# Projections of an attention kernel as four column-group products each, and the first key block's product in two halves

## The chip, the cores and the metric

The kernel runs on one core of a Trainium2 chip. The metric is the device time of one execution in microseconds; the median of three executions of the kernel before is 1588.9 us. Every profile and every time in this document is of that one core.

## What is computed

The reference is one "macaron" layer on an input of 8 sequences of 1024 tokens and 256 features, in float32: half a feed-forward block with experts, causal attention with 16 heads of 16 features, and another half feed-forward block, each behind a layer norm.

```python
x = L0_attn_x                                   # (8, 1024, 256)
x = x + 0.5 * _L0_ffn_ref(_layernorm(x, axis=-1), gate_w, w1, b1, w2, b2)
x = x + _L0_attn_ref(_layernorm(x, axis=-1), Wq, bq, Wkv, bkv, Wo, bo)
x = x + 0.5 * _L0_ffn_ref(_layernorm(x, axis=-1), gate_w, w1, b1, w2, b2)

def _L0_attn_ref(x, Wq, bq, Wkv, bkv, Wo, bo):
    q = x @ Wq.T + bq
    k, v = jnp.split(x @ Wkv.T + bkv, 2, axis=-1)
    q, k, v = (to_heads(q), to_heads(k), to_heads(v))
    dots = jnp.einsum('bhid,bhjd->bhij', q * scale, k)
    dots = jnp.where(causal, MASK_VAL, dots)
    attn = jax.nn.softmax(dots, axis=-1)
    out = jnp.einsum('bhij,bhjd->bhid', attn, v)
    return out.transpose(0, 2, 1, 3).reshape(b, n, d) @ Wo.T + bo

def _L0_ffn_ref(tokens, gate_w, w1, b1, w2, b2):
    cap = int(1.25 * N / E)
    probs = softmax(x @ gate_w.T); top2_w, top2_idx = top_k(probs, 2)
    counts = jnp.bincount(top2_idx.reshape(-1), length=E)
    keep = counts <= cap
    ...
```

An expert that is chosen more often than its capacity allows is dropped as a whole. The kernel counts the choices of both feed-forward blocks while it computes the attention, and works out a feed-forward block only in a branch that is taken where some expert is kept.

## The kernel before

In this profile the whole span is one call of `attention` (line 602). Its work is cut into 32 units: a unit `u` is one sequence `b` and one group `g` of four heads (`u = 4 b + g`). The loop at line 966 takes 24 steps for each unit. In every step TensorE gets, in this order:

- a score block (lines 991 to 996): two products `sc` of the unit `u` (keys against queries, for the exponential) interleaved with two products `sm` of the next unit (queries against keys, for the row maximum). All four contract 16 features in one of four row groups of 32 partitions, so that they run in the array at the same time; the profile writes this as 32*128. They are 512, 384, 256 or 128 columns wide. There are six PSUM banks for them (`score`, line 616), used in turn: a step's third product needs the bank that the first `sc` of the step before had, and its fourth the bank of the first `sm` of the step before. ScalarE (ACT) releases the first by its `Exp` into `pT`, VectorE (DVE) the second by its maximum.
- what is due of the products with v (lines 998 to 1003): `values(hf, jb, pTs, part)` (line 816). A product `pav` multiplies the exponentials of key block `jb` with v, four heads at once, each in one of four column groups of 32 output rows (128*32 in the profile). It is due two steps after its scores (`part` 0) and three steps after (`part` 1). Blocks of over 256 columns are divided in two parts, except for the first key block, whose 512 columns are all done in part 0; blocks of up to 256 columns are done in part 0 too. In the numbering of steps from 0 to 23, the first key block of the unit's first half of queries comes at step 3, that of the second half at step 11.
- one piece of other work (lines 1015 to 1022): at steps 2 and 12 `settle`, with four transposes `pm`; else the next piece of a queue, `even` at even steps and `odd` at odd ones.

The pieces of the two queues are made by generators. `enter` makes transposes `pta` of the normed input, `values_of` (line 678) one product `pv` a piece for v and the gate (264 columns, contracted over 256 features in two halves `c`), `project` (line 718) one product `pq` a piece for the keys or the queries of eight heads (512 columns, again two halves), and `leave` (line 860) one product `px` a piece for the output projection and the second gate (264 columns, two halves). These three kinds of projection use the full array of 128 by 128; so do the transposes. All of `pav`, `pv`, `pq`, `px`, `pm` and `pta` share the two PSUM banks of `bank` (line 620), one of which `pav` holds for about half a unit. A float32 product of TensorE shows as two weight loads and two matmuls in the trace.

The order of each engine's instructions is kept as written by `InOrder` (line 27), whose call at line 37 is why nearly all rows of the profile name line 37.

Of the kernel before, what the change touches and what calls it, by code (L numbers as in the profile page):

```python
# [18 lines left out]
P = 128  # L19
# [31 lines left out]
def macaron_kernel(  # L51
# [550 lines left out]
    def attention(run_no, src, dst, gate0, logits, tally):  # L602
# [3 lines left out]
        with stack:  # L606
# [20 lines left out]
            def matmul(out, lhsT, rhs, start=True, stop=True):  # L627
                pe.matmul(out, lhsT=lhsT, rhs=rhs, start=start, stop=stop)

            def transpose(out, in_, n=P):  # L630
                pe.transpose(out, in_, ident[:n, :n])

            xbs, xnTs, lns, stds, att_ds, qEs, gate_lns = {}, {}, {}, {}, {}, {}, {}


# [42 lines left out]
            def values_of(b):  # L678
                xb, xnT = xbs[b], xnTs[b]
                if gate0 is None:  # L680
                    lg = norm.tile([P, TB, E], F32, tag="lg", name=f"lg{b}")
                else:
                    lg = gate0[0][:, b * TB : (b + 1) * TB, :]
                for j in range(TB):
                    pv = bank(f"pv{b}_{j}")
                    for c in range(DC):
                        matmul(
                            pv[:, : D + E],
                            xnT[:, c, j * P : (j + 1) * P],
                            wvT[:, c, :],  # L690
                            start=(c == 0),
                            stop=(c == DC - 1),
                        )
                    vector.tensor_tensor(
                        vaugs[b % 2][:, j, : NH * VW].rearrange("p (h r) -> p h r", r=VW)[:, :, :HD],
                        pv[:, :D].rearrange("p (h r) -> p h r", r=HD),
                        bv_all.rearrange("p (h r) -> p h r", r=HD),
                        ALU.add,
                    )
                    vector.tensor_copy(lg[:, j, :], pv[:, D : D + E])  # L700
                    yield
                gpsimd.tensor_tensor(
                    xb[:, :, D:], lg, stds.pop(b).unsqueeze(2).to_broadcast([P, TB, E]), ALU.mult
                )
                for j in range(0, TB, 2):
                    part = xb[:, j : j + 2, :]
                    gpsimd.tensor_tensor(part, part, bo_all.unsqueeze(1).to_broadcast([P, 2, D + E]), ALU.add)
                    yield
# [9 lines left out]
            def project(u):  # L718
                b, g = divmod(u, NG)
                xnT = xnTs[b]  # L720
                gp = g // 2
                for s0 in range(0, S, 512):
                    for wT, bT, dsts, scale in ((wkT, bkT, kTs, 1.0), (wqT, bqT, qTs, QSCALE)):
                        pq = bank(f"pq{u}_{s0}")
                        for c in range(DC):
                            matmul(
                                pq,
                                wT[:, c, gp * P : (gp + 1) * P],
                                xnT[:, c, s0 : s0 + 512],
                                start=(c == 0),  # L730
                                stop=(c == DC - 1),
                            )
                        packed = ap.tile([P, 512], F32, tag="packed", name=f"packed{u}_{s0}", bufs=4)
                        scalar.activation(packed, pq, AF.Identity, bias=bT[:, gp : gp + 1], scale=scale)
                        for k in range(8):
                            r = 32 * (k % 4)
                            nc.sync.dma_start(  # L737
                                out=dsts[(u + k // 4) % 4][r : r + HD, s0 : s0 + 512],
                                in_=packed[HD * k : HD * (k + 1), :],
                            )  # L740
                        yield
# [44 lines left out]
            def e_steps(u):  # L786
                b, g = divmod(u, NG)
                kT = kTs[u % 4]
                pav = {}

                def scores(hf, jb, pr, out, h):
                    off = max(0, jb - 4 * hf) * P
                    w = 512 - off
                    r = 64 * pr + 32 * h
                    sc = score(f"sc{u}_{hf}_{jb}_{pr}_{h}")
                    matmul(sc[:, :w], kT[r : r + 32, jb * P : (jb + 1) * P], qEs[u, hf][r : r + 32, off:])
                    if h == 0:
                        out[pr] = ap.tile([P, 2, 512], F32, tag="pT", name=f"pT{u}_{hf}_{jb}_{pr}", bufs=8)
                    pT = out[pr]
                    scalar.activation(pT[:, h, :w], sc[:, :w], AF.Exp)  # L800
                    if h == 0:
                        return
                    if jb >= 4 * hf:
                        gpsimd.affine_select(
                            out=pT[:, :, :P],
                            in_=pT[:, :, :P],
                            pattern=[[0, 2], [1, P]],
                            compare_op=ALU.is_ge,
                            fill=0.0,
                            base=0,  # L810
                            channel_multiplier=-1,
                        )

                def values(hf, jb, pTs, part):
                    if jb == 0 and part == 0:
                        pav[hf] = bank(f"pav{u}_{hf}")
                    off = max(0, jb - 4 * hf) * P
                    w = 512 - off  # L820
                    if jb == 0 or w <= 256:
                        cols = slice(0, w)
                        if part == 1:
                            return
                    else:
                        cols = slice(part * w // 2, (part + 1) * w // 2)
                    for pr in (1, 0):
                        for h in range(2):
                            r = 64 * pr + 32 * h
                            v0 = (4 * g + 2 * pr + h) * VW  # L830
                            matmul(
                                pav[hf][r : r + 32, off + cols.start : off + cols.stop],
                                vaugs[b % 2][:, jb, v0 : v0 + 32],
                                pTs[pr][:, h, cols],
                                start=(jb == 0),
                                stop=(jb == 4 * hf + 3),
                            )
                    if jb == 4 * hf + 3 and part == 0:
                        att = ap.tile([P, 512], F32, tag="att", name=f"att{u}_{hf}", bufs=4)
                        scalar.copy(att, pav.pop(hf))  # L840
                        if g == 0:
                            att_ds[b, hf] = spill.tile(
                                [NH, 32, 512], F32, tag="att_d", name=f"att_d{run_no}_{b}_{hf}", bufs=3
                            )
                        nc.sync.dma_start(
                            out=att_ds[b, hf][4 * g : 4 * g + 4].rearrange("h r c -> (h r) c"), in_=att
                        )

                for hf in range(2):
                    for jb in range(4 * hf + 4):  # L850
                        pTs = {}
                        yield (lambda h, hf=hf, jb=jb, pTs=pTs: scores(hf, jb, 1, pTs, h)), None
                        yield (
                            (lambda h, hf=hf, jb=jb, pTs=pTs: scores(hf, jb, 0, pTs, h)),
                            (lambda part, hf=hf, jb=jb, pTs=pTs: values(hf, jb, pTs, part)),
                        )
# [3 lines left out]
            def leave(b, hf):  # L860
# [29 lines left out]
                for i in range(TB // 2):  # L890
                    j = hf * (TB // 2) + i
                    px = bank(f"px{b}_{j}")
                    for c in range(DC):
                        matmul(
                            px[:, : D + E],
                            on[:, c, i * P : (i + 1) * P],
                            woT[:, c, :],
                            start=(c == 0),
                            stop=(c == DC - 1),
                        )  # L900
                    vector.tensor_tensor(xb[:, j, :], px[:, : D + E], xb[:, j, :], ALU.add)
                    ln_stats(xb, j, *gate_lns[b])
                    yield
# [192 lines left out]
```

## Time and profile before

| | |
|---|---|
| median of three runs (lowest, highest) | 1588.9 us (1586.56, 1589.5) |
| the profiled execution's own time | 1588.83 us |
| its span, from the first to the last instruction | 1587.1 us |
| mean granted TensorE clock | 0.966 |
| matmuls of TensorE, and their weight loads | 11940 each |

The groups with the largest busy time of TensorE's projections and products with v, kept apart by shape (columns: line, engine, operation, output <- inputs, array tile, shape, count | busy us, mean ns of one | idle time before):

```profile
L37 PE MATMUL pav<-pT,vaug 128*32 128x256 f32 x2560 | 204.7, 391 | 0.0
L37 PE MATMUL pav<-pT,vaug 128*32 128x512 f32 x512 | 71.6, 632 | 0.1
L37 PE MATMUL pq<-xnT,wkT 128*128 128x512 f32 x128 | 63.5, 619 | 0.0
L37 PE MATMUL pq<-xnT,wqT 128*128 128x512 f32 x128 | 63.3, 617 | 0.0
L37 PE MATMUL pv<-wvT,xnT 128*128 128x264 f32 x256 | 76.3, 422 | 7.2 <-DVE logits L37 4.1 <-DVE xa L37 3.2
L37 PE MATMUL px<-woT,on 128*128 128x264 f32 x256 | 75.4, 419 | 16.3 <-POOL on L37 16.3
```

How to read it: matmuls run at the same time in different tiles and overlap in the pipeline, so a group's busy time is the time in which at least one of its matmuls is in the array[...]. Neither is the time that a block of matmuls costs. For that, the timeline is needed: the distance from the start of a block's first matmul to the start of the next block's first.

### The profile page before, as it was taken

What the parts mean: (1) busy time and instruction counts of PE and PEld (TensorE: products, weight loads), DVE (VectorE), ACT (ScalarE), POOL (GpSimd) and SP (SyncE); (2) the same over time, 40 slices, a digit from 0 to 9 for tenths busy, and PEclk for the clock granted to TensorE, in tenths of its full rate; (3) what the DMA queues carried; (4) which work ended last, traced back from release to release, by engine and by line L of the source; (5) the groups of instructions that cost most, each with busy time, mean ns of one, the idle gap of its engine ahead of it and who ended that gap; (6) DMA issues with size and microseconds to landing.
All of it is one profiled execution on the core that took longest, in us unless ns stands there. A gap on an engine that the chain in (4) does not pass through costs nothing.

```text
span 1587.1 us, 32518 instructions
## 1 busy us (share of the span) xinstructions
PE 1496.4 (94%) x11940; PEld 630.2 (40%) x11940; DVE 1120.9 (71%) x3519; ACT 764.3 (48%) x1722; POOL 332.6 (21%) x650
## 2 busy tenths in 40 slices
PE   4999999999999999999999999999999999999992
PEld 2444444344344434444344443334334443344431
DVE  4576777676867678676876768677686767767823
ACT  1045555454554455553554545554455535555560
POOL 3111212112121121223121131211212221112121
PEclk9779999999999999999999999999999999999996
DMA  4001111111111020211212111110302101121111
GB/s 126 13 14 28 37 32 45 46 36 54 55 50 49 27 74 23 61 49 32 64 34 56 36 49 52 50 49 21 87 22 62 42 23 46 36 62 36 34 36 57
DMA packets 58056, 71.69 MB, mean 45 GB/s; under 512 B 15640, under 2 KB 33312, under 8 KB 57888
## 3 DMA queue, kind: packets, MB, share of 16 engines
q1 hardware_dynamic: 55680, 68.20, 14.4%
q8 instruction: 96, 1.57, 0.4%
q10 hardware_dynamic: 2208, 1.32, 0.3%
q14 instruction: 72, 0.59, 0.1%
HBM read 27.01 MB, written 25.69 MB: 33 GB/s over the span
## 4 chain that ended last, share of the span: by engine, by line
PE 90%; DVE 6%; issue 1%; DMA 1%; SPq 1%; POOL 1%; ACT 0%; ACTq 0%; POOLq 0%
PE sc L37 39%; PE pav L37 20%; PE sm L37 10%; PE pq L37 7%; PE pv L37 5%; PE px L37 4%; PE pm L37 2%; DVE sm L37 2%; PE pta L37 1%; DVE first L37 1%; DVE xn_a L37 1%; SPq L737 1%; DMA xa<-in_L_attn_x_dram 0%; ACT pT L37 0%; DMA inv<-inv_d 0%
## 5 line engine op out<-in xcount | busy, mean ns | idle before, releaser
L37 ACT ACTIVATE pT<-sc 128x512 f32<-128x512 f32 (+3 forms) x1536 | 670.1, 490 | 637.1 <-PE sm L37 484.4
L37 PE MATMUL sm<-kT,qT 32*128 32x512 f32 (+3 forms) x3072 | 847.6, 545 | 13.7 <-DVE top L37 7.2
L37 PE MATMUL sc<-qE,kT 32*128 32x512 f32 (+3 forms) x3072 | 784.0, 541 | 1.0
L37 POOL TENSOR_SCALAR_AFFINE_SELECT pT<-pT 128x256 f32<-128x256 f32 x512 | 208.2, 408 | 1110.5 <-ACT pT L37 1106.6
L37 PEld LDWEIGHTS sc<-qE,kT 32*128 32x128 f32 x3072 | 285.7, 185 | 331.0 <-ACT pT L37 201.8
L37 DVE TENSOR_REDUCE first<-sm 128x1 f32<-128x512 f32 x512 | 329.1, 685 | 111.9 <-PE sm L37 99.5
L37 PE MATMUL pav<-pT,vaug 128*32 128x256 f32 (+3 forms) x4608 | 373.4, 396 | 0.1
L37 DVE CUSTOM_DVE_ANT_0 sm<-sm,causal 128x256 f32<-128x256 f32 (+3 forms) x512 | 241.5, 515 | 165.7 <-PE sm L37 164.9
L37 PEld LDWEIGHTS sm<-kT,qT 32*128 32x128 f32 x3072 | 329.3, 187 | 52.8 <-issue 18.5
L37 DVE CUSTOM_DVE_ANT_0 sm<-sm,causal,first 128x256 f32<-128x256 f32 (+3 forms) x512 | 261.7, 553 | 46.7 <-PE sm L37 31.0
L37 PEld LDWEIGHTS pav<-pT,vaug 128*32 128x32 f32 x4608 | 91.4, 108 | 298.9 <-issue 227.6
L37 DVE DVE_READ_ACCUMULATOR2_ANT top<- 128x1 f32 x1024 | 145.2, 142 | 0.0
L37 PE MATMUL px<-woT,on 128*128 128x264 f32 x256 | 75.4, 419 | 16.3 <-POOL on L37 16.3
L37 PE MATMUL pv<-wvT,xnT 128*128 128x264 f32 x256 | 76.3, 422 | 7.2 <-DVE logits L37 4.1
L37 DVE TENSOR_TENSOR xa<-px,xa 128x264 f32<-128x264 f32 x64 | 27.6, 432 | 58.3 <-PE px L37 56.5
L37 PE MATMUL pq<-xnT,wkT 128*128 128x512 f32 x128 | 63.5, 619 | 0.0
L37 PE MATMUL pq<-xnT,wqT 128*128 128x512 f32 x128 | 63.3, 617 | 0.0
L37 PEld LDWEIGHTS px<-woT,on 128*128 128x128 f32 x256 | 44.4, 193 | 47.3 <-POOL on L37 18.2
L37 PEld LDWEIGHTS pv<-wvT,xnT 128*128 128x128 f32 x256 | 44.7, 194 | 41.7 <-issue 10.9
L37 DVE TENSOR_TENSOR vaug<-pv,bv_all 128x256 f32<-128x256 f32 x64 | 27.1, 424 | 30.2 <-PE pv L37 28.8
L37 PE MATMUL pta<-ident,xn_a 128*128 128x128 f32 x128 | 23.2, 310 | 25.4 <-DVE xn_a L37 25.4
L37 DVE TENSOR_TENSOR qE<-qT,pm 128x512 f32<-128x512 f32 x64 | 43.6, 682 | 3.6 <-PE pm L37 3.6
(108 smaller groups left out, 595.3 us busy)
## 6 DMA issues: line engine op xcount, KB each, us to landing
att_d<-att SPq DMA_DIRECT2D x64, 256.0 KB
xa<-in_L_attn_x_dram SPq DMA_DIRECT2D x8, 1024.0 KB
kT<-packed SPq DMA_DIRECT2D x256, 32.0 KB
qT<-packed SPq DMA_DIRECT2D x256, 32.0 KB
on<-att_d SPq DMA_DIRECT2D x32, 256.0 KB
inv<-inv_d SPq DMA_DIRECT2D x32, 256.0 KB
out_dram<-xa SPq DMA_DIRECT2D x16, 512.0 KB
wsb<-in_L_attn_Wkv_dram ACTq DMA_DIRECT2D x2, 256.0 KB
```

Source lines behind the costliest of these rows:

```text
L37: i = call(*args, **kwargs)
L737: nc.sync.dma_start(out=dsts[(u + k // 4) % 4][r : r + HD, s0 : s0 + 512], in_=packed[HD * k : HD * (k + 1), :],)
```

## The change

A helper `matmul_cols` is added that issues a product as four, each for 32 of the 128 output rows; the four write the same PSUM bank at partitions 0, 32, 64 and 96. The three kinds of projection call it in place of `matmul`. In `values`, the first key block of 512 columns is no longer taken whole in part 0: columns 0 to 255 are done in part 0 and columns 256 to 511 in part 1, one step later; only part 0 carries the start flag.

```diff
+            def matmul_cols(out, lhsT, rhs, start=True, stop=True):
+                for r in range(0, P, 32):
+                    matmul(out[r : r + 32], lhsT[:, r : r + 32], rhs, start, stop)
...
                     for c in range(DC):
-                        matmul(
+                        matmul_cols(
                             pv[:, : D + E],
                             xnT[:, c, j * P : (j + 1) * P],
                             wvT[:, c, :],
...
                         for c in range(DC):
-                            matmul(
+                            matmul_cols(
                                 pq,
                                 wT[:, c, gp * P : (gp + 1) * P],
                                 xnT[:, c, s0 : s0 + 512],
...
                 def values(hf, jb, pTs, part):
...
-                    if jb == 0 or w <= 256:
+                    if w <= 256:
                         cols = slice(0, w)
                         if part == 1:
                             return
...
-                                start=(jb == 0),
+                                start=(jb == 0 and part == 0),
                                 stop=(jb == 4 * hf + 3),
...
                     for c in range(DC):
-                        matmul(
+                        matmul_cols(
                             px[:, : D + E],
                             on[:, c, i * P : (i + 1) * P],
                             woT[:, c, :],
```

TensorE's program grows by 1152 float32 products for the projections (192 projections of two halves, three more products for each half) and by 256 for the divided key block (two halves of queries in 32 units, four heads each). The instructions of the other engines and their order stay as they are.

## The prediction

> **What bounds the kernel now.** I read the page first, part 1 for the busy shares and part 4 for the chain, then the groups kept apart by shape, then TensorE's timeline.
>
> ```profile
> PE 1496.4 (94%) x11940; PEld 630.2 (40%) x11940; DVE 1120.9 (71%) x3519; ACT 764.3 (48%) x1722; POOL 332.6 (21%) x650
> PE 90%; DVE 6%; issue 1%; DMA 1%; SPq 1%; POOL 1%; ACT 0%; ACTq 0%; POOLq 0%
> PE sc L37 39%; PE pav L37 20%; PE sm L37 10%; PE pq L37 7%; PE pv L37 5%; PE px L37 4%; PE pm L37 2%; DVE sm L37 2%; PE pta L37 1%; DVE first L37 1%; DVE xn_a L37 1%; SPq L737 1%; DMA xa<-in_L_attn_x_dram 0%; ACT pT L37 0%; DMA inv<-inv_d 0%
> ```
>
> TensorE is the bound, and all three projections lie on the chain nearly whole: 7 + 5 + 4% of 1587 us is 254 us. [...] I need the distance from the first matmul of a block to the first of the next. The timeline gives it:
>
> ```profile
> 720.92 0.64 PE L37 MATMUL pav<-pT,vaug 128*32 128x256 f32 x8
> 721.49 1.16 PE L37 MATMUL px<-woT,on 128*128 128x264 f32 x4
> 722.58 0.58 PE L37 MATMUL sc<-qE,kT 32*128 32x384 f32 x1
> ...
> 646.47 1.06 PE L37 MATMUL pav<-pT,vaug 128*32 128x512 f32 x8
> 647.47 0.48 PE L37 MATMUL sc<-qE,kT 32*128 32x256 f32 x1
> ...
> 648.11 1.98 PE L37 MATMUL pq<-xnT,wqT 128*128 128x512 f32 x4
> 650.03 0.48 PE L37 MATMUL sc<-qE,kT 32*128 32x256 f32 x1
> ```
>
> A full-array px takes 1.09 us (721.49 to 722.58), a pq 1.92, four column-group products of 256 columns 0.57, of 512 columns 1.00. I took these distances over the whole trace, sorted by what stands before and after; they repeat to 1 or 2 ns: pav 356, 462, 569 and 996 ns for 128, 192, 256 and 512 columns; pv and px 1087; pq 1914.
>
> Every float32 product is two passes. The pav row is 139 ns + two passes of 1.67 ns a column (2 x 429 at 512, 2 x 215 at 256). For pq, 1914 = 198 + 4 x 429, with 429 the distance between its second, third and fourth matmul; for px, 1087 = 199 + 4 x 222. So four column groups stream at the full array's rate, all four at once, and the block's fixed part is 139 ns against 199.
>
> [...] a score block (32x128 tiles) between others costs 1070 ns, while one followed directly by another score block costs 962[...]. [...] In the trace the second pass starts 533 ns after the first in a 512-column score block (107 over the 427 of streaming), 453 in pav (26 over). [...]
>
> **The change part by part.**
>
> 1. Projection directly behind a pav in the same step. [...] Afterwards both have one mode and the projection should cost only its streaming, 4 x 222 = 888 or 4 x 429 = 1716: a gain of 199 each. Nearest row for such a chain: two score blocks with no other block between, where a tile's next product starts 429 ns after its last pass, nothing exposed. Counted in the program's order: 59 px, 36 pv, 17 pq = 112. 112 x 0.199 = 22.3 us.
>
> 2. Projection behind a score block: 199 becomes 139, 60 ns each. pq: 43 today, of which 14 get a pav ahead by part 4, so 29 x 0.06 = 1.7 us. pv: 8 x 0.06 = 0.5.
>
> 3. The six places at a unit's end where two pv follow px and wait for a bank (VectorE releases it): each starts its streaming 80 ns sooner, 12 x 0.08 = 1.0 us. The first four pq, the eight pv ahead of the first scores and the last four px stand beside VectorE and DMA waits; I take 0, at most 1 us.
>
> Does the gain survive? A score block's third matmul waits for ACT's exp of the score block before, its fourth for VectorE's reduction: the stall is set by the filler between two score blocks. In the trace, no filler gives a stall of about 860 to 970 ns at 512 columns, 586 ns of filler 270, 996 ns none. All fillers with a projection are at least 1.02 us afterwards, and today every score block after one has a stall of 0 to 2 ns. So the gain stays on the path. VectorE could come in where both takes of a step pair hold projections: in the unit at 719.85 to 734.10 it is busy 10.81 of 14.25 us, against six gains of 0.2.
>
> 4. The first key block's pav, 996 ns at steps 3 and 11 of a unit, becomes 569 there and 569 at steps 4 and 12, so TensorE pays 142 more; stalls move too. Cases over 31 units, sums of the two fillers and the stalls behind them (ns):
> - step 4 with nothing (10 units): before 996 - 108[...] + 764 = 1652; after 569 + 200 + 569 + 75 = 1413. Gain 0.24 each, 2.4 us. The 200 is ACT's and VectorE's 384-column work not yet done after 569 (the row with 586 before such a block has 204 to 207).
> - step 4 with pq (14): before 996 + 1914 = 2910; after 569 + 200 + 569 + 1716 = 3054. Loss 0.144, 2.0 us.
> - step 4 with pta (7): before 996 + 586 + 70 = 1652; after 569 + 200 + 569 + 585 = 1923. Loss 0.27, 1.9 us.
> - step 11 without px (23): before 996 + 586 (pm) + 270 = 1852; after 569 + 270 + 569 + 585 = 1993. Loss 0.14, 3.2 us. The transposes of pm come 142 ns later; the qE that VectorE makes of them is not read for ten steps.
> - step 11 with px (7), its 199 counted in 1: the pm stall of 270 goes, 142 is added. Gain 0.13, 0.9 us.
> Sum: a loss of 3.8 us.
>
> VectorE's, ACT's, POOL's and SP's instructions and their order are the same; pT of key block 0 is held one step longer, with eight buffers and one used a step, which costs nothing.
>
> Bounds for what the trace does not show. The chain pav to projection: full gain 22.3[...]. Sixteen column products reading one moving operand in four streams: pav's four streams are different data, so equality is not shown; I take equality. The split: at best the stall after step 3 is 0 (6 us better), at worst VectorE lags and it is 427 (7 us worse). I take the middle.
>
> Net: -22.3 - 1.7 - 0.5 - 1.0 + 3.8 = -21.7 us. The span 1587.1 becomes 1565.4, and the profiled execution's own time 1588.83 becomes 1567.1; the median of the runs, 1588.9, is the same to 0.1.
>
> **Rivals.**
>
> A, the gain is halved. For: with VectorE 71% busy and no idle time in some steps (2, 3 and 13 of many units), a step shortened by 0.2 hands part of it to the next stall; and matmuls come denser. [...] afterwards steps with 128-column scores, pav and pv hold 32 matmuls in about 1.78 us, 56 ns each. Against: pav of 128 columns already has eight in 356 ns, 45 each, and 512-column steps are at 79. Price: some 10 us, 1577.
>
> B, slower. Each burst of four column products pays the block's fixed part for itself, because the second half of the sum (c = 1) writes the bank's same rows as the first. Then a pv or px is 2 x (139 + 444) = 1166 instead of 1087, a pq 2 x (139 + 858) = 1994 instead of 1914: +0.08 on some 190 projections, 15 us, and the split loses its shared mode with 14 pq (+2.8 over 3.8): 1588.8 + 15 + 6.6 = 1610. It decides against the change from an extra 0.12 us per projection on (21.7 / 188). For it: no column chain over eight products is in the trace. Against: the score chain of eight products, and the second pass in each pav, which adds to the same rows 429 ns after the first.
>
> C, the change doesn't do what it says: four products with the same moving operand run one after the other. Then pv and px grow by 3 x 888 and pq by 3 x 1716 ns: 128 x 2.66 + 64 x 5.15 = 670 us, about 2260. Against: the four tiles of pav start 7 ns apart.
>
> **How the numbers follow.** Forecast 0.66 (own range 1559 to 1575), A 0.16, B 0.13, C 0.01, and 0.04 that gains and losses cancel. A measurement of this kernel tells about 0.2% (3 us) from no change. Faster: forecast and A, 0.82; same 0.04; slower 0.14. Range 1559 to 1582 takes in A and the unknown ends.
>
> **What would show it.** Distance from px to the next score block behind a pav near 890 ns, pq near 1716; pq behind scores near 1855. Steps 4 and 12 with a pav of 569; stall at step 12 near 270 and at 13 near 0. A first matmul of c = 1 more than 240 ns after the second pass of c = 0 in the same group shows B. Stalls over 50 ns behind projections show A. If the px blocks come out at 890 and the time has not fallen by 15 us, my reading of the stalls is wrong.

## The result, and the profile after

The changed kernel takes 1573.6 us (median of ten, 1564.49 to 1578.89) against 1588.5 for the kernel before; the ratio is 0.9889, with a 95% interval from 0.9852 to 0.9926. The profiled execution took 1565.43 us, its span is 1563.7 us at a mean granted clock of 0.968. The ten executions fall into two groups, five from 1564.5 to 1569.3 us at a clock of 0.965 to 0.968 and five from 1577.9 to 1578.9 at 0.958 or 0.959, so the profile stands for the faster group and the median lies between the two (experiment 4 asks what separates them).

Page of the kernel after, part 1 and both lines of part 4:

```profile
PE 1473.4 (94%) x14756; PEld 601.3 (38%) x14756; DVE 1124.1 (72%) x3519; ACT 764.4 (49%) x1722; POOL 333.3 (21%) x650
PE 89%; DVE 7%; issue 1%; DMA 1%; SPq 1%; POOL 1%; ACT 0%; ACTq 0%; POOLq 0%
PE sc L37 40%; PE pav L37 21%; PE sm L37 10%; PE pq L37 7%; PE pv L37 4%; PE px L37 4%; PE pm L37 2%; DVE sm L37 2%; PE pta L37 1%; DVE first L37 1%; DVE xn_a L37 1%; SPq L743 1%; DMA xa<-in_L_attn_x_dram 0%; DVE key_g L37 0%; DVE cand_g L37 0%
```

2816 more matmuls, and TensorE is busy for 23 us less. The shares of the chain are nearly those of before: the bound did not move, it became cheaper. Where, the timeline of TensorE in the kernel after shows (start us, length us, engine, line, operation, count):

```profile
711.23 0.64 PE L37 MATMUL pav<-pT,vaug 128*32 128x256 f32 x8
711.69 1.07 PE L37 MATMUL px<-woT,on 128*32 128x264 f32 x16
712.69 0.58 PE L37 MATMUL sc<-qE,kT 32*128 32x384 f32 x1
...
638.04 0.64 PE L37 MATMUL pav<-pT,vaug 128*32 128x256 f32 x8
638.49 1.90 PE L37 MATMUL pq<-xnT,wqT 128*32 128x512 f32 x16
640.33 0.48 PE L37 MATMUL sc<-qE,kT 32*128 32x256 f32 x1
```

From pav to the next score block it is now 1.46 us with a px between (1.66 before), and 2.29 with a pq. The px starts only 0.46 us after pav where it was 0.57. Score blocks of 512 columns show nearly the same step in the trace of before: 962 ns where another score block follows directly, 1070 where a block of another mode does. A mode here is the array tile that the profile prints, such as 128*32.

Executions also differ in how long TensorE ran at half clock; a stretch in which the trace shows a granted clock of 0.5 is called a dip below. To compare kernels without the dips I use a second number, the undisturbed time of units 2 to 30. It is the sum, over these units, of the distance from the unit's first score matmul to that of the next unit. A unit that a dip touches counts with the median of the untouched units of the same `g` in sequences 1 to 6 (of 0 to 7); these agree within 0.02 us, though in some traces only one of a `g` is untouched. The undisturbed time is 1318.6 us before and 1297.8 after, 20.8 less. Units 0 and 1 hold dips of nearly the same length in both traces and add 1.9, so the gain in units 0 to 30 is 22.7 us. To take off half of every dip instead would mislead: in units 5, 9 and 25 of the kernel before, 6.8 us at half clock cost 2.57 us and not 3.4, since TensorE waits in part of them anyhow.

### The profile page after: what moved, and what is told of

It is laid out like the page before. It is cut to its first block, busy times and chain, and to the rows that moved or that the text cites. A ratio compares the mean times of both kernels' runs of the same rounds, so it can differ in the third digit from the quotient of the medians.

```text
span 1563.7 us, 38156 instructions
## 1 busy us (share of the span) xinstructions
PE 1473.4 (94%) x14756; PEld 601.3 (38%) x14756; DVE 1124.1 (72%) x3519; ACT 764.4 (49%) x1722; POOL 333.3 (21%) x650
## 4 chain that ended last, share of the span: by engine, by line
PE 89%; DVE 7%; issue 1%; DMA 1%; SPq 1%; POOL 1%; ACT 0%; ACTq 0%; POOLq 0%
PE sc L37 40%; PE pav L37 21%; PE sm L37 10%; PE pq L37 7%; PE pv L37 4%; PE px L37 4%; PE pm L37 2%; DVE sm L37 2%; PE pta L37 1%; DVE first L37 1%; DVE xn_a L37 1%; SPq L743 1%; DMA xa<-in_L_attn_x_dram 0%; DVE key_g L37 0%; DVE cand_g L37 0%
## 5 line engine op out<-in xcount | busy, mean ns | idle before, releaser
L37 PE MATMUL pav<-pT,vaug 128*32 128x256 f32 (+2 forms) x5120 | 385.7, 373 | 0.1
L37 PEld LDWEIGHTS pav<-pT,vaug 128*32 128x32 f32 x5120 | 101.3, 108 | 334.4 <-issue 259.1
L37 PE MATMUL px<-woT,on 128*32 128x264 f32 x1024 | 70.8, 396 | 16.2 <-POOL on L37 16.2
L37 PE MATMUL pv<-wvT,xnT 128*32 128x264 f32 x1024 | 71.6, 398 | 7.7 <-DVE logits L37 4.3
L37 PE MATMUL pq<-xnT,wkT 128*32 128x512 f32 x512 | 61.8, 601 | 0.0
L37 PE MATMUL pq<-xnT,wqT 128*32 128x512 f32 x512 | 61.1, 595 | 0.0
L37 PEld LDWEIGHTS px<-woT,on 128*32 128x32 f32 x1024 | 33.1, 112 | 39.7 <-POOL on L37 18.3
L37 PEld LDWEIGHTS pv<-wvT,xnT 128*32 128x32 f32 x1024 | 31.3, 111 | 42.0 <-issue 7.1
L37 ACT ACTIVATE packed<-pq,bqT 128x512 f32<-128x512 f32 x32 | 22.0, 687 | 47.5 <-PE pq L37 38.5
```

The lines of the kernel that those rows point to most:

```text
L37: i = call(*args, **kwargs)
```

## The experiments

**1. The two parts of the change, each alone.** The first kernel keeps the column groups and leaves the first key block's product whole:

```diff
-                    if w <= 256:
+                    if jb == 0 or w <= 256:
...
-                                start=(jb == 0 and part == 0),
+                                start=(jb == 0),
```

> Projections in column groups, first key block's product left whole. Theory (the gain is the shared tiling mode[...]): 112 projections behind a pav save 0.199 us, 51 behind scores 0.060, the pairs at a unit's end 1.0 in all: a span 26.4 us under that of before, 1560.7. A px behind a pav adds 890 ns to it, a pq behind scores takes 1855. Rival (the divided key block brings a good part of the gain, by filling steps that had no filler): a span over 1570.

The second is the kernel before with those two lines the other way, and its projections in the full array.

> First key block's product divided, projections left in the full array. Theory: 62 times 142 ns more of TensorE time, stalls that move rather than go, and no shared mode with the pq of step 4: 3 to 7 us slower than before, a span of 1590 to 1594. Rival (dividing evens out the steps): faster than before by 3 us or more.

Column groups alone: 1571.2 us, ratio 0.991 (0.9878 to 0.9941), profiled span 1569.5 at a clock of 0.961. In the trace every block is as expected: px adds 890 ns to a pav (456 + 1003, against 569), a pq behind scores takes 1854. But the span is 9 us over the forecast and, read alone, within 0.5 us of what the rival said. Most of that is the clock: there are ten dips between 150 and 1520 us, where before has seven. Set against untouched units, the dips of units 2 to 30 cost 15.3 us here and 13.0 before, and unit 0, which holds dips in both, lasts 2.7 us longer. The undisturbed time is 1296.6, 22.0 under before, with units 0 and 1 some 24 (an estimate, as the dips in unit 0 differ); 26.4 were expected for the whole span. The divided block alone: 1593.3 us, ratio 1.0024 (1.0002 to 1.0046), a profiled span of 1594.5, just over the range given, and an undisturbed time of 1321.8, 3.2 over before. So the column groups bring the whole gain and the divided block costs. Alone it costs 3.8 us by its own timed runs (0.24% of 1589) and 3.2 undisturbed. Beside the column groups it costs 1.2 (1297.8 - 1296.6), because the 14 pq at step 4 then stand behind a pav and save 198 ns instead of 60. The timed runs of the first kernel and of the change itself overlap and do not rank these two.

**2. Shared mode or short weight loads.** Two products of 64 rows in place of four of 32:

```diff
-                for r in range(0, P, 32):
-                    matmul(out[r : r + 32], lhsT[:, r : r + 32], rhs, start, stop)
+                for r in range(0, P, 64):
+                    matmul(out[r : r + 64], lhsT[:, r : r + 64], rhs, start, stop)
```

> As the change, but each projection as two products of 64 output rows, which is another tiling mode than that of pav (four groups of 32). Theory (most of the gain is the mode shared with pav): [...] fixed part near 150 ns in place of 199, so about 8 us gained on the projections and 6 lost on the divided block: a span of 1583 to 1588. Rival (the gain is the shorter weight load and the overlap of groups, in any column mode): a span under 1575.

In the traces a weight load of px lasts 190 ns before and 110 after (medians). Measured: 1572.2 us, ratio 0.9922 (0.9892 to 0.9951), a profiled span of 1569.9. By the time alone, both theories miss and the rival's is the nearer. TensorE's timeline of this kernel says otherwise:

```profile
713.37 0.64 PE L37 MATMUL pav<-pT,vaug 128*32 128x256 f32 x8
713.93 1.11 PE L37 MATMUL px<-woT,on 128*64 128x264 f32 x8
714.98 0.58 PE L37 MATMUL sc<-qE,kT 32*128 32x384 f32 x1
```

The pav ahead of px is back at 0.56 (0.57 before, 0.46 in the change) and px costs 1041 ns, 153 + 888, where the forecast, an estimate of mine, was "near 150". Counted by kind of block outside the dips (the median distance of each kind, times how often it stands there), the projections gain 46 or 47 ns each, 7.8 us in units 0 to 30, where four groups gain 26.6. The undisturbed time is 1314.8, 3.8 under before, so the divided block takes back about half of the 7.8. The rest of the time came from elsewhere: this execution has a single dip of the clock between 110 and 1500 us, before has eight, and those of units 2 to 30 cost it 13.0 us. So a column mode other than pav's is worth 7.8 us here; the mode shared with pav carries most of the other 18.8, since a projection behind a pav keeps a fixed part of 153 ns with 64 rows and, with 32, costs its streaming alone (890 ns for a px that streams 888). That its clock is better is not explained by the edit; 11 of its 17 executions are at 0.975 or above, those of before and after at 0.955 to 0.971.

**3. The order of the small products.** The loop over row groups outside, the two halves of the sum inside:

```diff
-                for r in range(0, P, 32):
-                    matmul(out[r : r + 32], lhsT[:, r : r + 32], rhs, start, stop)
+                for r in range(0, P, 32):
+                    for c in range(DC):
+                        matmul(out[r : r + 32], lhsTs[c][:, r : r + 32], rhss[c], c == 0, c == DC - 1)
```

> As the change, but with the loop over the 32 output rows outside and that over the two halves of the sum inside, so that both halves of a row group stand one behind the other in the program. Theory (each tile works through its own products, whatever stands between them): px behind pav stays at 890 ns and the span within 3 us of 1563.7. Rival (TensorE takes its queue in order, and a product for a busy tile holds up those behind it): the groups no longer run at the same time for part of each projection, and px takes 1.3 us or more, the span 1640 or more.

Measured: 1582.4 us, ratio 0.9941 (0.9915 to 0.9967). Its timeline:

```profile
721.87 0.64 PE L37 MATMUL pav<-pT,vaug 128*32 128x256 f32 x8
722.34 1.11 PE L37 MATMUL pv<-wvT,xnT 128*32 128x264 f32 x16
723.38 0.69 PE L37 MATMUL sc<-qE,kT 32*128 32x512 f32 x1
```

Both theories miss. The 1.3 us of the rival did not come; but a pv block behind a pav takes 1040 ns and its pav 469, 50 ns more than in the change's order, and a projection behind a score block 20 more. Counted by kind of block and outside the dips, that is 7.3 us over the changed kernel in units 0 to 30. Why the order matters by this much was not tried. It is worth having the four groups of one half stand together.

**4. What the clock does.** The spread within the ten executions first. This profile of experiment 3 had a head like that of the longer executions: its first full step (scores of both units) begins at 96.6 us where that of the change begins at 84.4. A window of the change, then of experiment 3 (us, busy time and count of PE, PEld, DVE, ACT, POOL, then the mean TensorE clock, DMA share, GB/s):

```profile
61.00:88.00 27.00, 26.72 (x173) 13.80 (x166) 23.90 (x74) 0.90 (x2) 5.36 (x5) 0.81 0.00 1
```

```profile
61.00:88.00 27.00, 27.00 (x133) 8.68 (x126) 12.40 (x27) 0.00 (x0) 2.30 (x3) 0.51 0.00 1
```

In the head TensorE waits for inputs (in the change 12.2 us for `xn_a` from VectorE and 7.3 for the transfers of the weights `wsb`) and runs at half clock for 23.9 us, or in experiment 3 for 51.2: 27 us more at half speed are some 13 us. That is near the 12.2 us by which the first full step is later, and near the distance between the two groups of the change (1565 and 1578.5). Of the ten profiles of this document three have such a head (first full step at 95.9 to 96.6 us), the others begin that step at 83.0 to 85.1. Of the ten runs of before beside the change, two lie some 13 us above the others, at 1601. That the long executions of the change itself have this head is inferred from the size; none of them was profiled.

Now the dips further on. The timeline of the kernel after, and its windows there:

```profile
676.13 0.59 PE L37 MATMUL sm<-kT,qT 32*128 32x512 f32 x1
678.70 1.09 PE L37 MATMUL pta<-ident,xn_a 128*128 128x128 f32 x4 [1.99 <-DVE xn_a L37]
679.72 1.22 PE L37 MATMUL sc<-qE,kT 32*128 32x512 f32 x1
```

```profile
675.00:678.70 3.70, 1.72 (x20) 0.50 (x17) 2.61 (x10) 1.53 (x4) 0.87 (x3) 1.00 0.00 0
678.70:682.10 3.40, 3.40 (x20) 1.41 (x20) 1.05 (x4) 0.80 (x2) 0.00 (x0) 0.50 0.00 0
```

TensorE idles 1.99 us until VectorE has normed two tiles of the next sequence, and then runs at half clock for 3.4 us: a score matmul takes 1.22 us in place of 0.69. To take that wait away I issued the norm of these tiles ahead of the scores, in the kernel before and in the changed one:

```diff
                 normed(0)
+                yield
                 for jj in range(TB // 2):
...
                     entering = chain(enter(b + 1), values_of(b + 1))
+                    next(entering)
```

> The kernel before, with the norm of a sequence's first two tiles issued ahead of the scores of step 0 in units with g = 1, so that the transposes there wait for nothing. Theory (the granted clock falls to 0.5 for 3.4 or 6.8 us after a stretch in which TensorE was nearly idle): the 1.9 us idle gaps ahead of pta go, some 1.8 us in each of 7 units or 12 us in all, and with them the dips that began 2 to 4 us behind them (six of the nine dips after 110 us in the kernel before, some 12 us lost): a span of 1560 to 1566, no dip within 6 us behind a first pta. Rival (dips come with time or load, whatever TensorE's gaps): as many dips as before, a span near 1574.

> The same edit on the changed kernel. Theory: the gaps of 2.0 us go (12 us) and the dips behind them (two of eight in the profile of after, 3 us); the dips behind step 10 of units with g = 2, where VectorE works on the gate, stay: a span of 1546 to 1552. With the clock's loss taken off on both sides, 17 to 22 us less than the kernel before with this edit; if the change's gain were an effect of the dips, that difference would be under 8 us.

On the kernel before: 1577.2 us, ratio 0.9918 (0.989 to 0.9946), where a span of 1560 to 1566 was expected. Its profiled execution was the longest of its runs (span 1591.5, clock 0.955, with the long head), so only positions and untouched units are read from it. No dip stands within 6 us behind a first pta any more, as expected, and a unit with g = 1 lasts 51.53 us in place of 53.25: 12 us over seven units, what the waits held. But the dips of units 2 to 30 still cost 13.4 us, against 13.0. They now follow two other lean places: the stall behind step 10 of units with g = 2 (as at 400.1 and 587.8 us), and a 0.94 us gap (420.6, 608.3 and 977.0 us). The kernel before has this gap six times, and never a dip behind it. Between 110 and 1500 us there are eight dips, as many as before, which is what the rival said; their places speak for the theory "a dip follows a lean stretch", whose conclusion that their number would fall was wrong. The kernel before has 19 such lean stretches (seven at pta, six gaps of 0.94 us, six stalls of 2.6 us at step 10), and which of them is followed by a dip changes with the edit.

On the changed kernel: 1551.3 us, ratio 0.9776 (0.9711 to 0.9841). The difference between the two kernels with this edit is the test of the change: undisturbed 1308.1 - 1287.4 = 20.7 us, against 20.8 without the edit. By the timed medians it is 26, by the lowest times 17. The gain is not an effect of the dips.

**5. A filler where there was none.** On the changed kernel, the second pq of a unit with g = 0 or 2 moves from step 6 to step 10:

```diff
-                    elif k % 2 == 0:
+                    elif k % 2 == 0 and not (k == 6 and u >= 0 and g % 2 == 0):
                         take(even)
-                    else:
+                    elif k % 2 == 1:
                         take(odd if odd or 0 <= u < NU - 1 else even)
```

> The changed kernel, with the second pq of units with g = 0 and 2 at step 10, which had no filler, instead of step 6, which has a pav. Theory (the stall of a score block is what the filler ahead of it leaves over): at step 6 1716 ns go, at step 10 1854 come and a stall of 966 (g = 0) or up to 2629 (g = 2) goes: about 0.7 us in 8 units and 1.6 in 6, 15 us, and the dips behind step 10 of g = 2 with them, up to 8: a span of 1540 to 1549. Rival (the stall at step 10 is VectorE's or ACT's lag and comes back one step later): within 3 us of 1563.7.

Measured: 1561.3 us, ratio 0.982 (0.9763 to 0.9877), a profiled span of 1563.5, exactly the rival's; but that execution had the long head and a clock of 0.958. The stalls decide: behind step 10 of the 14 units they are 0 to 184 ns, where in the changed kernel 23 steps 10 without a filler had 965 to 2664. A part came back in the units with g = 2: at step 7 about 540 ns in six of them and 1963 in unit 2, and at step 10 itself 500 in place of 90. The undisturbed time is 1286.4, 11.4 under the changed kernel, where 15 were expected for the stalls: 0.83 us in each of seven units with g = 0, 1.19 in six with g = 2 (0.7 and 1.6 expected), and unit 2 lasts 1.7 longer. The 8 us hoped for from dips did not come: 9.8 us are lost to them in units 2 to 30, against 10.5.

**6. Together.** Both edits, and the first key block divided only where the prediction's ledger had a gain:

```diff
-                    if w <= 256:
+                    halve = jb > 0 or (hf == 0 and (g == 3 or (b == B - 1 and g > 0))) or (hf == 1 and g == 0 and b > 0)
+                    if w <= 256 or not halve:
```

> Both edits together on the changed kernel, and the first key block divided only where step 4 had nothing (g = 3, and the last sequence) or where step 11 has a px (g = 0). Theory: the gains add up, 12 + 15 + 4 for the divided blocks left whole, and hardly a dip after 150 us: a span of 1520 to 1532. Rival (removing one wait brings the next forward): over 1540.

Measured: 1528.6 us, ratio 0.9633 (0.9568 to 0.9698), faster than both kernels. Its profiled span is 1523.5 us. Part 1 of its page, and a window from 110 to 1480 us:

```profile
PE 1449.0 (95%) x14380; PEld 583.5 (38%) x14380; DVE 1118.3 (73%) x3519; ACT 764.7 (50%) x1722; POOL 333.5 (22%) x650
```

```profile
110.00:1480.00 1370.00, 1354.03 (x13746) 537.74 (x13744) 1032.42 (x3238) 742.97 (x1673) 303.08 (x598) 1.00 0.16 47
```

The undisturbed time is 1271.4, 47.2 under before and 26.4 under the changed kernel: 10.3 and 11.4 for the two edits, which leaves 4.7 for the blocks that stay whole (4 expected). So the gains add up, and the rest is the clock: this execution has no dip at all between 110 and 1480 us.

## Why the prediction was right

It said 1567.1 us for an execution like the profiled one; the profile is 1565.43, and the median of 1573.6 lies in the range. The mechanism of its main term, the mode shared with pav, is in the trace; the sizes of two smaller terms were off, and their errors partly cancel.

The chain from pav to projection: 569 + 888 = 1457 ns forecast for pav and px, 1459 measured; 569 + 1716 = 2285 for pav and pq, 2286; 1855 for pq behind scores, 1854. Between two blocks of one mode no fixed part shows (1459 - 569 = 890 ns for px, 888 of them streaming), and four streams of one operand run like four of different ones: behind scores the second pass of a pq starts 453 ns after its first, as in a 512-column pav of before. (The prediction's 1.67 ns a column is for both passes of a product together.) Counted by kind of block and outside the dips, all fillers of the units 0 to 30 together fell by 17.7 us. The terms of the prediction add up to 18.9 there: 22.3 + 1.7 + 0.5 + 1.0 for the projections, less 0.6 for three px of unit 31, and 14 x 0.198 = 2.8 for the pq at step 4, less 62 x 0.142 = 8.8. Most of the difference is its part 3: at the six places where two pv follow a px, the run from pav to the end of the pv became 216 ns shorter, where 199 + 160 were forecast.

That the gain survives: behind every projection in a step the score block stalls for 0 to 2 ns, but for one at 168. Rival A, a gain handed on to the next stall, is not seen.

The divided block: at steps 4, 5 and 13 the stalls moved as forecast. Forecast were +7.3, -7.4 and -8.1 us, measured +6.3, -8.0 and -8.3 (the first figure of each with the 1.1 us that ten score blocks now pay, 108 ns each, since a pav follows them and not another score block). At step 12 the forecast was +6.2, a stall of 270 ns in 23 units, and outside the dips it is +2.5: 287 ns in seven units, 84 in six, none in the other ten. Here are steps 11 to 13 of one of the seven, first before, then after:

```profile
707.75 1.07 PE L37 MATMUL pav<-pT,vaug 128*32 128x512 f32 x8
708.75 0.69 PE L37 MATMUL sc<-qE,kT 32*128 32x512 f32 x1
...
708.76 0.69 PE L37 MATMUL sc<-qE,kT 32*128 32x512 f32 x1
...
709.82 0.66 PE L37 MATMUL pm<-ident,top 128*128 128x128 f32 x4
710.40 0.69 PE L37 MATMUL sc<-qE,kT 32*128 32x512 f32 x1
...
710.62 0.69 PE L37 MATMUL sc<-qE,kT 32*128 32x512 f32 x1
710.70 0.69 PE L37 MATMUL sm<-kT,qT 32*128 32x512 f32 x1
```

```profile
698.16 0.64 PE L37 MATMUL pav<-pT,vaug 128*32 128x256 f32 x8
698.73 0.69 PE L37 MATMUL sc<-qE,kT 32*128 32x512 f32 x1
...
698.96 0.69 PE L37 MATMUL sc<-qE,kT 32*128 32x512 f32 x1
699.04 0.69 PE L37 MATMUL sm<-kT,qT 32*128 32x512 f32 x1
...
700.09 0.64 PE L37 MATMUL pav<-pT,vaug 128*32 128x256 f32 x8
700.66 0.66 PE L37 MATMUL pm<-ident,top 128*128 128x128 f32 x4
701.25 0.69 PE L37 MATMUL sc<-qE,kT 32*128 32x512 f32 x1
...
701.26 0.69 PE L37 MATMUL sc<-qE,kT 32*128 32x512 f32 x1
```

The late third and fourth products (0.22 and 0.30 behind the first) stand at step 13 before and at step 12 after: the stall changed its place, and 142 ns were added. And here is step 12 of unit 26 after, one of the ten in which it does not stall:

```profile
1305.34 0.64 PE L37 MATMUL pav<-pT,vaug 128*32 128x256 f32 x8
1305.91 0.69 PE L37 MATMUL sc<-qE,kT 32*128 32x512 f32 x1
...
1305.92 0.69 PE L37 MATMUL sc<-qE,kT 32*128 32x512 f32 x1
1305.93 0.69 PE L37 MATMUL sm<-kT,qT 32*128 32x512 f32 x1
```

What the prediction missed. First, it priced the stalls by the filler alone. A score block whose third and fourth products came late lets ACT and VectorE start early on its first two, so the next block stalls less; this reading fits the stalls, but was not tried alone. Where step 10 has no filler, the block of step 11 is late by 965 ns or more, and that of step 12 then stalls for 85 ns at most: 3.7 us better than forecast. After, the block of step 13 is not late, and that of step 14 stalls 288 ns in place of 154 in 23 units: 3.1 us worse. Steps 15 to 18 give 0.7 back. Beside the column groups the divided block therefore costs 1.2 us (experiment 1), not 3.8.

Second, the dips, which no term has. Before, most of them stand behind the first pta of units with g = 1, after at steps 11 and 12 of units with g = 2; set against untouched units, those of units 2 to 30 cost 13.0 us before and 10.5 after. So the 23.4 us by which the profiled span fell are 22.7 of gain in units 0 to 30 and 2.5 of cheaper dips, less 1.8 by which what stands ahead of unit 0 and behind unit 30 grew. The ledger for these units was 21.1 (21.7 less the 0.6 of unit 31). The projections gave about 1 us less than it says and the divided block cost some 2.6 less; that these errors, the dips and the two ends leave the forecast within 2 us of the profile is in part luck. Third, the median: the prediction carried the profile's gain over to it one to one, and half of the executions of the change came out 13 us longer.

Rival B is refuted by the chain of 1459 ns, and by its own sign: the first matmul of c = 1 starts 222 ns after the second pass of c = 0, not more than 240. Rival C falls by the same chain.

## What to carry to other kernels

Price a block of matmuls by the distance from its first start to the next block's, and split it into a part that streams and a fixed part. Here the fixed part of a projection was 199 ns in the full array; with four groups of 32 rows it was 138 behind a score block (1854 - 1716) and hardly there behind a pav, whose mode it shares (890 - 888); in a column mode of its own (64 rows) a projection behind a pav kept 153 of the 199. The score buffers are freed by other engines: in the kernel before, a block of 512 columns stalled 860 to 970 ns with no filler ahead of it, 270 behind a filler of 586 and not at all behind one of 996, so put work into the steps that have none before evening out those that have some. When kernels differ by 1%, set the granted clock beside the time before a theory is believed or dropped, and compare stretches of work that no dip touches: here three of the eight kernels looked like their rivals until that was done.

## What the runs showed of the hardware that was not expected

TensorE's granted clock fell to 0.5 for 3.413, 6.827 or 10.240 us in six to eleven places between 110 and 1500 us of every profile but the best version's and that with 64 rows (none and one). Of these 68 dips, 67 begin at most 4.1 us after the start of a stretch of 1.18 to 2.58 us in which no matmul starts; for the one at 1469.7 us in experiment 5 I found no such stretch. Each of these nine traces has 12 to 19 such stretches there, so the 4.1 us behind them are at most 6% of the time; but the one with 64 rows has 19 of them and a single dip. Why a dip follows one of them and not another was not tried; the same gap (the 0.94 us one of experiment 4) was followed by a dip in one kernel and not in the next. A sequence of this kernel lasts 184 to 188 us, and dips often return at that distance (385.1, 569.4, 753.8, 938.1 and 1122.4 us in the profile of after). In the head the first stretch at half clock is 24, 51 or 65 us long, and the longer ones make the first full step some 12 us later. In units 2 to 30 the dips cost 0 to 15.3 us of a 1570 us kernel; where to put the lean stretches so that no dip follows was not tried either.
